# Graph attention, then relational attention: scores of two graphs at a time as four row tiles, and DRAM trips emitted in two steps

## The chip, the cores and the metric

The kernel runs on one core of one Trainium2 chip. The metric is the device time in microseconds of one execution. Before the change it is 2887.8 us, the median of three runs (2886.82, 2887.80 and 2892.35).

## The reference

128 graphs of 128 nodes with 256 features go through two layers. Everything is f32.

- Layer 0: two graph attentions, each a masked softmax of 128x128 additive scores and a product with `h W`; the residual and a layer norm; a feed-forward of 256 to 1024 to 256 with relu; a second norm.
- Layer 1: eight heads of 32 features. The weights of the softmax are masked by relation, and every relation has values of its own:

```
q = src @ Wq + bq; k = src @ Wk + bk           (8 heads of 32)
attn = softmax(q k^T / sqrt(32))
out = sum over r of (attn * (adj == r)) @ (src @ Wv[r] + bv[r])
x = norm(src + out @ Wo + bo)
y = norm(x + gelu(x @ W1 + b1) @ W2 + b2)
```

The adjacency is 0 or 1 in these inputs. The kernel looks for a larger value at its start and has an arm for each case. Here the arm called BINARY runs: the values of relation 0 are applied to all weights, and those of relation 1 less relation 0 to the masked ones, so two products per head remain.

## The kernel before

Graphs are worked on in 32 groups of four (`G`), with the 128 nodes of a graph on the partitions. Every group passes five stages: `load`, `gat` (both graph attentions), `ff0`, `att` (layer 1's attention), `ff1`.

**What sets the order of the work.** Each stage is a Python generator. It emits some instructions and then yields a number of units, which are planned time and not measured time. `layers` (L598) keeps all running stages in a heap by planned time: the stage `k` of group `g` starts at `100 g + begin[k]` (load -87, gat -51, ff0 48, att 132, ff1 300), and each yield puts it back by that many units. So five groups are interleaved, and the pattern repeats every 100 units. The numbers stand in `TIMES` (L30). TensorE (PE) executes in the order of emission from unit 280 on, and SP's queue, which issues every DMA, does so from the start (`kept`, L57). The other engines' order is made by a scheduler at compile time; each of their instructions is placed no earlier than the PE instruction emitted before it. Every engine then takes its own queue in order.

**The trip through DRAM.** To turn 128x128 blocks round, `transposed` (L273) lets VectorE (DVE) transpose 32x32 blocks in place (L288), stores them with four DMAs of 128 KB to a DRAM tile (L291) and loads that tile back with one DMA of 512 KB (L293), in which the blocks stand in their new places. It does the three in one go. In SP's queue the load therefore stands right behind its stores, waits for their landing, and all that is emitted later waits with it. There are seven such trips a group: the features ahead of ff0, att and ff1, and four graphs' weights of attention. `gat_weighting` (L393) has a smaller trip of the same kind (L405, L407). The first and last groups use transposes on PE in some places instead (`direct`, L282).

**PSUM.** Of eight banks, one holds the output `av` of the weighted values, and seven are a pool called `mm` for every other product.

**Attention** (L459). q and k are computed for a group at a time, 512 tokens. ScalarE (ACT) writes k twice for each half of the features into `kbd` (L476), with 32 rows of each 64 set to zero by `own`: a key tile that is block-diagonal over pairs of heads. `weights(b)` (L483) makes the scores of one graph: for each half of the features, two row tiles of 64 rows run side by side, each giving two heads in 256 columns, into two banks. DVE takes the row maxima (L496), ACT the exponentials with their sums (L500), DVE the reciprocals (L501), GpSimd (POOL) the division (L502). `turned` makes the trip. `by_relation` masks (L515), `values` (L525) makes the values and `weighted` (L536) multiplies them with four column tiles of 32 columns; ACT copies the result out (L548), and `wo` (L577) follows. Graph by graph: two graphs' weights are started ahead, and those of graph b+2 are emitted right behind the values of graph b.

**The other stages.** `feed_forward` (L315) computes its first product in eight visits by seven block products in place of eight (L333) and its second product in two halves (L378). A visit of a new unit takes two banks, `chain` and `side`; the second product takes two.

Of the kernel before, what the change touches and what calls it, by code (L numbers as in the profile page):

```python
# [31 lines left out]
    "ff first half": 10, "ff half": 5, "row": 16, "gat": 19, "wh": 5.5,  # L32
    "gat copy": 2, "qk": 4.5, "scores": 5.5, "turn0": 10, "turn1": 5,
    "v0": 5.5, "av": 9, "v": 4, "wo": 4, "turn": 3, "mask": 3,
    "lead ff0": 26, "lead att": 32, "lead ff1": 32, "affine": 7,
# [5 lines left out]
    binary=False, times=TIMES, period=430, bufs=dict(T=3, tok=2, m=4, mm=6, v=1),  # L41
    begin=dict(load=-87, gat=-51, ff0=48, att=132, ff1=300), early={},
# [4 lines left out]
    binary=True, times=TIMES,  # L47
    period=100, bufs=dict(T=5, tok=5, m=1, mm=7, v=2),
# [37 lines left out]
def constants(tc, a, c, cst, tmp, ps):  # L86
# [59 lines left out]
    def others():  # L146
# [16 lines left out]
        c.kbd = [cst.tile([P, G, 2, P], F32, name=f"kbd{n}") for n in range(DC)]  # L163
        c.own = cst.tile([P, 2], F32, name="own")
        nc.vector.memset(c.own, 0.0)
        for q in range(P // Q):
            nc.vector.memset(c.own[ts(q, Q), q % 2:q % 2 + 1], 1.0)
        c.bk_own = [cst.tile([P, DC], F32, name=f"bk{q}") for q in range(2)]
# [52 lines left out]
def stages_of(tc, a, out, c, pools, plan):  # L221
# [51 lines left out]
    def transposed(y, t, direct, z):  # L273
# [4 lines left out]
        if direct:  # L278
# [8 lines left out]
            return  # L287
# [5 lines left out]
        nc.sync.dma_start(t, s.rearrange("k p i t -> p k (i t)"))  # L293
# [4 lines left out]
    def features(y, direct):  # L298

        t = t_tile().rearrange("p (b c n) -> p b c n", b=G, c=DC)  # L300
        blocks = t.rearrange("p b c n -> p (b c) n")
        transposed(y.rearrange("p b (c f) -> p (b c) f", f=P), blocks, direct, blocks)
        return t
# [11 lines left out]
    def feed_forward(y, before, direct, win, bin_, wout, func, by=G):  # L315


        hT = features(y, direct)
# [75 lines left out]
    def gat_weighting(wh, k, cap, direct):  # L394
# [6 lines left out]
        else:  # L401
# [4 lines left out]
            p = e  # L406
            nc.sync.dma_start(p, bass.AP(tensor=s.tensor, offset=s.offset, ap=[[0, P], [1, G * N]]))  # L407
# [51 lines left out]
    def attention(y, g, first, direct):  # L459

        hT = features(y, first or direct)
        at = load_mask(g)
        yield TIMES["lead att"]
        qT = t_tile().rearrange("p (c t) -> p c t", c=DC)
        for i in range(DC):
# [4 lines left out]

        for i in range(DC):
            p = ps.tile([P, G, N], F32, name="mm")
            for f in range(DC):
                nc.tensor.matmul(p, c.wk[:, f, ts(i, P)], hT[:, :, f], start=f == 0, stop=f == DC - 1)  # L474
            for q in range(2):
                nc.scalar.activation(c.kbd[i][:, :, q], p, AF.Identity, scale=c.own[:, q:q + 1],  # L476
                                     bias=c.bk_own[q][:, i:i + 1])
# [5 lines left out]
        def weights(b):  # L483


            scores = [ps.tile([P, DC, 2, N], F32, name="mm") for _ in range(2)]
            for i in range(DC):
                for h in range(2):
                    rows = ts(h, P // 2)
                    nc.tensor.matmul(scores[h][:, i], qT[rows, i, ts(b, N)], c.kbd[i][rows, b],  # L490
                                     start=True, stop=True, tile_position=(h * P // 2, 0))
            e = wk.tile([P, H, N], F32, name="e1")
            for h, p in enumerate(scores):
                p = p.rearrange("p c q n -> p (c q) n")
                nm = sm.tile([P, HC], F32, name="nm1")
                nc.vector.tensor_reduce(nm, p, AX.X, OP.max, negate=True)  # L496
                s = sm.tile([P, HC], F32, name="s1")
                eh = e[:, ts(h, HC)]
                for q in range(HC):
                    nc.scalar.activation(eh[:, q], p[:, q], AF.Exp, bias=nm[:, q:q + 1], accum_out=s[:, q:q + 1])  # L500
                nc.vector.reciprocal(s, s)  # L501
                nc.gpsimd.tensor_mul(eh, eh, per_row(s, N))  # L502
            return e
# [279 lines left out]
```

## Time and profile before

| | |
|---|---|
| median of three runs | 2887.8 us |
| the profiled execution | 2891.83 us, of which span 2890.0 us |
| PE busy | 2787.7 us (96%) |
| ACT, POOL, DVE busy | 1724.3, 1597.4, 1504.7 us |
| share of the DMA engines, main queue | 49.1% |
| granted TensorE clock, mean | 0.982 |

The profile is of one execution. A row of a timeline has the start and the length in us, the engine, the line of the kernel, the operation, what is written from what, the shapes (for PE: rows and columns of the array, then the data) and the number of records; in brackets stands how long the engine was idle before it and what ended that. An f32 matmul is two records. Lengths of matmuls contain their latency, so their pace is read from one start to the next. In the list of waits each line has who waited, for what, the total in us, how often and the longest. SP's rows are DMAs issued, and their length is the time to issue them.

### The profile page before, as it was taken

Reading aid. Unit: us, or ns where it says so; the run is one execution under the profiler, and the core shown is the slowest. Engines: PE = TensorE matmul, PEld = TensorE weight load, DVE = VectorE, ACT = ScalarE, POOL = GpSimd, SP = SyncE. Lnnn points to the kernel's source line nnn. Section 1 sums busy time; section 2 is a strip of 40 time slices with the busy share of each in tenths; the row PEclk is TensorE's granted clock in tenths of the full one; section 3 lists DMA queues with packets and bytes.
Section 4 is the critical chain, followed back from the end, with each engine's and each line's share of the span. In section 5 each row is a group of like instructions: output and inputs, shape, how many; then the busy total and the mean of one; then the engine's idle time right before and its main releaser. Section 6 shows DMA issues by size and latency. Waiting matters only on the chain.

```text
span 2890.0 us, 45554 instructions
## 1 busy us (share of the span) xinstructions
PE 2787.7 (96%) x15554; PEld 2166.1 (75%) x15554; DVE 1504.7 (52%) x3072; ACT 1724.3 (60%) x5191; POOL 1597.4 (55%) x1866
## 2 busy tenths in 40 slices
PE   4996999999999999999999999999999999999988
PEld 3764777777877777777777787777778777777756
DVE  5444545545545555554554555555565545555442
ACT  3445566566666666666656666666666675666543
POOL 1434556556655556665655665565566565556553
PEclk7998999999999999999999999999999999999999
DMA  7145454555554556555445545454654544564310
GB/s 275 45 104 121 104 118 106 110 132 127 119 114 107 113 117 139 114 119 118 106 108 131 129 113 125 104 111 117 137 128 107 123 106 111 122 135 106 77 37 15
DMA packets 1156945, 328.69 MB, mean 114 GB/s; under 512 B 903008, under 2 KB 1126752, under 8 KB 1156064
## 3 DMA queue, kind: packets, MB, share of 16 engines
q1 hardware_dynamic: 1156704, 325.68, 49.1%
q8 instruction: 126, 2.06, 0.3%
q14 instruction: 115, 0.94, 0.1%
HBM read 195.97 MB, written 129.62 MB: 113 GB/s over the span
## 4 chain that ended last, share of the span: by engine, by line
PE 71%; DMA 7%; DVE 6%; POOL 5%; ACT 4%; issue 2%; SPq 2%; DVEq 0%; POOLq 0%; ACTq 0%
PE mm L378 25%; PE mm L333 19%; PE mm L531 5%; PE mm L474 4%; PE mm L468 4%; PE mm L490 4%; PE av L544 3%; PE mm L435 3%; PE mm L577 3%; POOL tok L271 2%; DMA zd<-e 2%; SPq L291 2%; DMA eT<-zd 2%; PE mm L454 1%; DMA zd<-T 1%
## 5 line engine op out<-in xcount | busy, mean ns | idle before, releaser
L271 POOL TENSOR_TENSOR tok<-tok,ln_rows 128x512 f32<-128x512 f32 (+1 forms) x596 | 669.5, 1133 | 34.4 <-PE mm L282 11.1
L500 ACT ACTIVATE e<-mm,nm 128x128 f32<-128x128 f32 x1024 | 362.1, 397 | 239.2 <-DVE nm L496 229.6
L378 PE MATMUL mm<-w,fT 128*128 128x256 f32 x2048 | 460.6, 381 | 0.0
L378 PE MATMUL mm<-wf,fT 128*128 128x256 f32 x2048 | 456.6, 381 | 1.5 <-ACT fT L354 1.5
L378 PEld LDWEIGHTS mm<-w,fT 128*128 128x128 f32 x2048 | 386.6, 190 | 74.2 <-issue 24.2
L502 POOL TENSOR_TENSOR e<-e,s 128x512 f32<-128x512 f32 x256 | 269.4, 1053 | 300.5 <-DVE s L501 299.8
L378 PEld LDWEIGHTS mm<-wf,fT 128*128 128x128 f32 x2048 | 386.5, 190 | 64.3 <-issue 9.2
L515 DVE TENSOR_TENSOR m<-eT,am 128x1024 f32<-128x1024 f32 x128 | 186.2, 1454 | 385.2 <-DMA eT<-zd 374.8
L496 DVE TENSOR_REDUCE nm<-mm 128x4 f32<-128x512 f32 x256 | 162.9, 676 | 254.6 <-PE mm L490 254.6
L265 ACT ACTIVATE tok<-tok,nmr,rstd 128x256 f32<-128x256 f32 x480 | 249.9, 603 | 20.1 <-POOL nmr L263 20.0
L531 PE MATMUL mm<-wv,T 128*128 128x512 f32 x512 | 249.3, 610 | 0.0
L352 POOL TENSOR_TENSOR fT<-fT 128x512 f32<-128x512 f32 x128 | 163.3, 1277 | 153.8 <-ACT fT L351 153.8
L500 ACT ACTIVATION_READ_ACCUMULATOR e<-mm,nm 128x1 f32 x1024 | 242.9, 237 | 0.0
L354 ACT ACTIVATE fT<-fT,col 128x512 f32<-128x512 f32 x256 | 170.4, 715 | 118.8 <-DVE fT L348 117.1
L309 POOL TENSOR_TENSOR t<-T 128x256 f32<-128x256 f32 x64 | 47.6, 744 | 321.3 <-DMA T<-zd 321.0
L333 PE MATMUL mm<-T,w 128*128 128x256 f32 x768 | 202.3, 386 | 4.0 <-DMA T<-zd 2.9
L424 POOL TENSOR_TENSOR e<-e,s 128x512 f32<-128x512 f32 (+1 forms) x68 | 68.1, 1002 | 244.4 <-DVE s L423 230.6
L333 PE MATMUL mm<-T,wf 128*128 128x256 f32 x768 | 193.1, 381 | 0.0
L256 DVE BATCH_NORM_STATS2 st<-tok 128x6 f32<-128x256 f32 x480 | 176.7, 409 | 2.4
L333 PEld LDWEIGHTS mm<-T,w 128*128 128x128 f32 x768 | 144.4, 192 | 30.6 <-issue 6.5
L422 ACT ACTIVATE e<-e,nm 128x128 f32<-128x128 f32 x256 | 101.6, 430 | 105.2 <-DVE nm L419 98.8
L333 PEld LDWEIGHTS mm<-T,wf 128*128 128x128 f32 x768 | 146.1, 191 | 21.7 <-issue 0.8
(144 smaller groups left out, 5147.1 us busy)
## 6 DMA issues: line engine op xcount, KB each, us to landing
zd<-e SPq DMA_DIRECT2D x496, 128.0 KB, 4.6
eT<-zd SPq DMA_DIRECT2D x124, 512.0 KB, 4.4
zd<-T SPq DMA_DIRECT2D x364, 128.0 KB, 3.5
T<-zd SPq DMA_DIRECT2D x91, 512.0 KB, 4.2
xt<-in_xT_dram SPq DMA_DIRECT2D x32, 512.0 KB, 5.0
e<-zsd SPq DMA_DIRECT2D x60, 256.0 KB, 3.3
tok<-in_x_dram SPq DMA_DIRECT2D x30, 512.0 KB
out_dram<-tok SPq DMA_DIRECT2D x29, 512.0 KB, 5.4
```

Source lines behind the costliest of these rows:

```text
L256: nc.vector.bn_stats(st, y[:, b])
L265: nc.scalar.activation(y[:, b], y[:, b], AF.Identity, bias=nmr[:, b:b + 1], scale=rstd[:, b:b + 1])
L271: engine.tensor_tensor(y[:, b:b + n], y[:, b:b + n], v[:, None, :].to_broadcast([P, n, D]), op)
L333: nc.tensor.matmul(p[:, i], win[k][:, ts(f0 + i, P)], hs[k], start=first and i == 0, stop=True, skip_group_check=True)
L352: nc.gpsimd.tensor_add(hi[:, :, 1], hi[:, :, 1], hi[:, :, 0])
L354: nc.scalar.activation(lo[:, i], lo[:, i], func, bias=bin_[:, f0 + i:f0 + i + 1])
L378: nc.tensor.matmul(ys[b // 2][:, b % 2], fT[f][:, ts(b, N)], wout[:, f], start=b % 2 == 0 and n == 0, stop=n == FC - 1, skip_group_check=True)
L496: nc.vector.tensor_reduce(nm, p, AX.X, OP.max, negate=True)
L500: nc.scalar.activation(eh[:, q], p[:, q], AF.Exp, bias=nm[:, q:q + 1], accum_out=s[:, q:q + 1])
L502: nc.gpsimd.tensor_mul(eh, eh, per_row(s, N))
L515: nc.vector.tensor_tensor(m, eT, at[:, b][:, None, :].to_broadcast([P, H, N]), OP.mult)
L531: nc.tensor.matmul(p, hT[:, b, f], wv[:, f, r:r + 2], start=f == 0, stop=f == DC - 1)
```

## The change

Three things change.

1. **Scores.** The key tile is plain: `kT`, one copy per half of the features. `weights(bs)` takes several graphs, two in the BINARY arm (`together=2`). Each matmul has 32 rows and 128 columns, and four row tiles stand side by side, one head each. Head q of a half writes to bank q, which holds two graphs and both halves, so a pair of graphs takes four banks. Four reductions of 128x512 are followed by sixteen exponentials; one reciprocal and one division of 128x1024 follow per graph. The order of the heads in the weights is now the natural one.
2. **Pairs.** The values, masks, output projection and `av` also go by two graphs. The scores of the second pair are emitted right behind the weighted values of the first. The buffers of `m` become two and that of `oT` one, of twice the size.
3. **Two steps.** `transposed` becomes `put` (transpose and stores) and `get` (load). `put` is emitted, 7 units pass, then `get`; for the second graph of a pair 3 more. The gat's small trip is divided by 5 units. The lead times become shorter by as much.

The other arm, GENERAL, which doesn't run here, gets one graph at a time, a longer period and a later ff1.

```diff
-    "ff first half": 10, "ff half": 5, "row": 16, "gat": 19, "wh": 5.5,
-    "gat copy": 2, "qk": 4.5, "scores": 5.5, "turn0": 10, "turn1": 5,
-    "v0": 5.5, "av": 9, "v": 4, "wo": 4, "turn": 3, "mask": 3,
-    "lead ff0": 26, "lead att": 32, "lead ff1": 32, "affine": 7,
+    "ff first half": 10, "ff half": 5, "row": 11, "gat": 19, "wh": 5.5,
+    "gat copy": 2, "qk": 7, "scores": 14, "mask": 4, "av": 8, "wo": 8, "turned": 6,
+    "put": 7, "next put": 3, "row put": 5,
+    "lead ff0": 19, "lead att": 25, "lead ff1": 25, "affine": 7,
...
-    period=100, bufs=dict(T=5, tok=5, m=1, mm=7, v=2),
+    period=100, bufs=dict(T=5, tok=5, m=2, mm=7, v=2),
...
+        return s
+
+    def get(t, s):
+        if s is not None:
+            nc.sync.dma_start(t, s.rearrange("k p i t -> p k (i t)"))
...
-        transposed(y.rearrange("p b (c f) -> p (b c) f", f=P), blocks, direct, blocks)
+        s = put(y.rearrange("p b (c f) -> p (b c) f", f=P), blocks, direct, blocks)
+        yield TIMES["put"]
+        get(blocks, s)
...
+            yield TIMES["row put"]
             nc.sync.dma_start(p, bass.AP(tensor=s.tensor, offset=s.offset, ap=[[0, P], [1, G * N]]))
...
-            for q in range(2):
-                nc.scalar.activation(c.kbd[i][:, :, q], p, AF.Identity, scale=c.own[:, q:q + 1],
-                                     bias=c.bk_own[q][:, i:i + 1])
+            nc.scalar.activation(kT[:, i], p, AF.Identity, bias=c.col["bk"][:, i:i + 1])
...
+        def weights(bs):
+            n = len(bs)
+            scores = [ps.tile([P, n, DC, N], F32, name="mm") for _ in range(HC)]
+            for j, b in enumerate(bs):
+                for i in range(DC):
+                    for q in range(HC):
+                        rows = ts(q, DH)
+                        nc.tensor.matmul(scores[q][:, j, i], qT[rows, i, ts(b, N)], kT[rows, i, ts(b, N)],
+                                         start=True, stop=True, tile_position=(q * DH, 0))
...
+        def turned(es):
+            eT = [wk.tile([P, H, N], F32, name="eT") for _ in es]
+            stored = [put(e, t, direct, e) for e, t in zip(es, eT)]
+            yield TIMES["put"]
+            for n, (t, k) in enumerate(zip(eT, stored)):
+                if n:
+                    yield TIMES["next put"]
+                get(t, k)
             return eT
...
+        STEP = plan["together"]
         yield TIMES["qk"]
+        es = weights(range(STEP))
         yield TIMES["scores"]
+        eT = yield from turned(es)
+        for b in range(0, G, STEP):
+            bs = range(b, b + STEP)
+            vs = [values(k) for k in bs]
+            affine(y, "02", b, STEP)
+            yield TIMES["mask"]
+            parts = [(by_relation(k, e, range(R)), v) for k, e, v in zip(bs, eT, vs)]
             yield TIMES["av"]
+            oT = weighted(parts)
+            if b + STEP < G:
+                es = weights(range(b + STEP, b + 2 * STEP))
             yield TIMES["wo"]
...
+            if b + STEP < G:
+                yield TIMES["turned"]
+                eT = yield from turned(es)
```

## The prediction

> **What bounds the kernel now.** I read the page first: its engine lines, then the 40 slices.
>
> ```profile
> span 2890.0 us, 45554 instructions
> PE 2787.7 (96%) x15554; PEld 2166.1 (75%) x15554; DVE 1504.7 (52%) x3072; ACT 1724.3 (60%) x5191; POOL 1597.4 (55%) x1866
> PE   4996999999999999999999999999999999999988
> ```
>
> TensorE (PE) is full in all slices but the first, the fourth and the last two. A busy share can hide slow matmuls, so I took stretches and then the timeline of PE.
>
> ```profile
> 1000.00:1200.00 200.00, 199.35 (x1118) 156.49 (x1117) 109.35 (x227) 125.74 (x381) 119.72 (x140) 1.00 0.56 124
> 2800.00:2890.00 90.00, 71.17 (x353) 56.43 (x352) 25.88 (x53) 36.00 (x78) 33.94 (x44) 0.89 0.09 24
> ```
>
> (PE, its weight loads, DVE, ACT, POOL, then granted clock, DMA share, GB/s.) In the middle PE idles 0.65 us of 200.
>
> ```profile
> 1063.27 7.07 PE L378 MATMUL mm<-w,fT 128*128 128x256 f32 x32
> 1070.27 1.13 PE L490 MATMUL mm<-kbd,T 64*128 64x256 f32 x8
> 1071.33 0.43 PE L544 MATMUL av<-eT,v 128*32 128x128 f32 x8
> 1071.57 0.40 PE L544 MATMUL av<-m,v 128*32 128x128 f32 x8
> 1072.34 1.13 PE L490 MATMUL mm<-kbd,T 64*128 64x256 f32 x8
> 1073.40 3.72 PE L378 MATMUL mm<-w,fT 128*128 128x256 f32 x16
> 1076.96 1.03 PE L333 MATMUL mm<-T,wf 128*128 128x256 f32 x4
> ```
>
> Starts matter here. Each f32 matmul is two records. A full 256-column record takes 0.2155 us (elsewhere in this answer four of L333 start 0.86 to 0.87 apart). The 32 of L378 take 6.90, and the next start is 7.00 later, so going to a tiled mode costs 0.10. One graph's scores (L490) take 1.06: four pairs of records at 0.216, about 0.10 for the first weights, which nothing hides, and 0.09 of mode change. One graph's values (L544) take 1.01: eight steps of four column tiles at 0.109, 0.03 first weights, 0.09 change. Back in full mode 16 records take 3.56 and not 3.45: 0.11 for exposed weights. PE therefore runs at its own pace, and groups follow each other every 85.1 us (L468 starts at 1056.4 and, a group on, at 1141.4). Last, the waits.
>
> ```profile
> DVE m L515 <- DMA eT<-zd: 374.8, 92, 9.4
> PE av L544 <- DMA eT<-zd: 14.6, 2, 12.0
> SPq L293 <- DMA zd<-e: 327.3, 245, 3.1
> ```
>
> DVE and SP wait long for the trips through DRAM, but PE waited for them only twice, at the ends of the program: the order of emission leaves room.
>
> [...] The trace agrees for two row tiles (two records per 0.216 us); four are not in it. [...] 64-row loads (L490) last 187 ns, 128-row ones (L378) 190, and loads with almost nothing beside them repeat thus:
>
> ```profile
> L192 PEld LDWEIGHTS mm<-col,w 128*128 128x128 f32 x32 | 3.7, 192 | 0.1
> ```
>
> That is 0.112 us each, once the last one's tail is taken off. [...]
>
> **The change part by part, per group of four graphs.**
>
> *Scores.* Before: 4 x 1.06 = 4.24 us. After, a pair is 16 matmuls, 32 records, in 8 steps of four row tiles with 128 columns. A step streams 128 columns (0.109, as in L544) over weights that take 0.112 to load: 0.112. A pair: 8 x 0.112 + 0.10 + 0.09 = 1.09; two, 2.18. Saved 2.06. Bounds: 0.109 a step (saved 2.10), or only two tiles at once, 0.216 (two pairs 3.84, saved 0.40). I take four at once, since row and column tiles already run two and four at once.
>
> *Values and bursts.* Matmuls stay. Before 4 x 1.01 = 4.04; after 2 x (16 x 0.109 + 0.12) = 3.73: saved 0.31. The same timeline, over a whole group, has four tiled bursts (at 1011.7, 1030.4, 1048.2, 1070.3), each costing 0.10 in and 0.11 after; walking the new times gives three: saved 0.2. Output projection and v only change places.
>
> Together **2.57 us a group** of PE.
>
> *Other engines.* Two kbd copies per half (128 of 774 ns) become one kT copy: 49 us less ACT. Reciprocals halve; exponentials, elements of the reductions and POOL's products stay. POOL's affine step goes by two graphs: 1.375 us in place of twice 0.77. None is on the path: PE at 99.7% hides ACT at 60%, POOL and DVE at 55%. Were ACT the bound, the copies would be worth 49/32 = 1.5 us a group.
>
> *Trips.* SP issues the same DMAs. It now runs on past the stores instead of sitting for their landing (327 us for zd<-e alone), so stores of others, xt loads and row trips go earlier; the load stands behind whatever 5 to 7 units emit, the 512 KB output store among it (0.6 us of SP). The lead times keep their sums (7+19=26, 7+25=32, 5+11=16). PE waits for none of these now: nothing gained. Two trips now stand close; the timelines of SP and of DVE give their price:
>
> ```profile
> 1084.28 2.56 SPq L291 DMA_DIRECT2D zd<-e  x4
> 1089.56 0.38 SPq L293 DMA_DIRECT2D eT<-zd  x1
> 1090.04 4.46 SPq L291 DMA_DIRECT2D zd<-e  x4
> 1096.85 0.38 SPq L293 DMA_DIRECT2D eT<-zd  x1
> ```
>
> ```profile
> 1083.02 1.24 DVE L288 STREAM_TRANSPOSE e<-e 128x1024 f32<-128x1024 f32 x1
> ...
> 1093.80 1.85 DVE L515 TENSOR_TENSOR m<-eT,am 128x1024 f32<-128x1024 f32 x1 [2.59 <-DMA eT<-zd]
> ```
>
> Stores take 5.3 us from issue until the load may go (1084.28 to 1089.56), 6.8 when the first load is in their way (1090.04 to 1096.85); a load takes 4.2 (1089.56 to the mask at 1093.80).
>
> *The pair's chain, the new danger.* PE executes in order of emission, so what counts is the PE work between a pair's scores and its values. In units from its group's start, the first pair's scores are emitted at 132+7+25+7 = 171 and its values at 171+14+7+3+4+8 = 207; the second pair's scores follow there, its values at 207+8+6+7+3+4+8 = 243. The other stages repeat every 100 units: the next group's ff0 (from 148) emits the second halves of its second product at 216 and 221, the gat of the group after it (from 149) its last product at 232, the previous group's ff1 (from 200) its first three visits at 237, 239.5 and 242. So between the second pair's scores and values stand: scores with changes 1.2, output projection 8 records 1.72, ff0 32 records 6.90, v of two graphs 8 records of 0.429, 3.43, gat 8 records 1.72, visits of 8, 8 and 12 records 6.03, change 0.09: **21.1 us**. Before it was 35.5 (1012.72 to 1048.20 in the timeline). For the first pair the same walk gives 32. The chain, from the scores' start: scores 1.2; first reduction 0.65; 16 exponentials at 0.35 (eight of L500 go from 1072.15 to 1074.91), 5.6; reciprocal and a product of 1024 elements, twice L502's 1.05 and 0.3, 2.4; transpose 1.2: 11.1 for the second graph. Its stores 5.3 to 6.8, load 4.2, mask 1.2: 21.8 to 23.3. It is needed 0.9 after the first graph's values begin, so the start is allowed at 20.9 to 22.4. PE waits 0 to 1.3 us, and what stands ahead on DVE, ACT or POOL (the gat softmax, a normalisation: up to 2 us, as the mask of 1.85 for 1.22 shows) comes on top: 0 to 3.3. I take 1.0. Behind the waiting matmul PE is in order, so all of it is lost.
>
> *Banks.* Four score banks are held until the sixteen exponentials end. With two of the second product's, six of seven are taken when a feed-forward visit wants two: 0 to 1 us, taken 0.2. The gat rows now queue behind eight stores on SP, with 27 us of PE work to hide them: 0 to 1, taken 0.2. The projection stands 1.2 us behind its values, for ACT's copy of 0.6: 0 to 0.5, taken 0.
>
> *Sum.* 2.57 - 1.4 = 1.17 us a group. From 288 to 2760 us PE is full over 29 periods: 34 us. Start and tail have idle PE and a longer chain by pairs: taken 0, bounds -5 and +8. The profiled execution, 2891.8 (span 2890.0 and 1.8 around it), would be 2858; it stands 4.0 above the median, so **2854**.
>
> **Rivals.** *No stall*: the chain fits; 32 x 2.57 = 82, so 2806 to 2830. For it: the minimum 20.9 is under 21.1, and PE stalls before are 0.2 us a group. Against: any queueing breaks it. *The second pair's values become the bound*, the slower case: eight stores in a row and busy engines bring the operand later than 21.1 + 2.57 = 23.7 us after the scores; from there on the change loses. At 25 it loses 1.3 + 0.4 us a group, 49 us: 2937. For it: the stores of 6.8 us and a DMA share of 0.56; against: the fixed terms end at 22.4. *Row tiles run two at a time*: saved 0.40 + 0.31 + 0.2 = 0.91 less 1.4, 14 us slower: 2902. *Stall eats the gain exactly*: 2888.
>
> **How the numbers follow.** Forecast (2831 to 2880) 0.46; no stall 0.18; gain eaten, within 0.2% (5.8 us, about what a measurement here can tell), 0.07; the chain bound 0.22; two tiles 0.07. Faster 0.64, same 0.07, slower 0.29. The range 2812 to 2905 leaves out about 0.05 below (nothing reaches far under 2806) and 0.14 above. [...]
>
> **What would show it.** Score records of 32 rows, eight per 0.112 us step counting loads, a pair in 1.1; three bursts a group; periods of 83.9. PE idle before the second pair's values, released by the mask or the load eT<-zd, near 1 us; over 2.6 and I am wrong in sign. A step of 0.216 breaks the gain; PE waiting elsewhere, for a bank, means I misplaced the stall. SP's wait for zd<-e should fall well under 327 us without moving PE.

## The result, and the profile after

The changed kernel takes 3101.1 us (median of four runs, 3098.6 to 3105.7) against 2889.2 us (2886.8 to 2892.4): 1.073 times as long, 95% interval 1.0716 to 1.0753. It is 212 us slower, where 2854 us, 34 us faster, was predicted.

The page of the changed kernel begins so (span, engines, PE in 40 slices, then the granted clock in the same slices):

```profile
span 3103.9 us, 46881 instructions
PE 2797.4 (90%) x16578; PEld 2188.5 (71%) x16578; DVE 1505.7 (49%) x2873; ACT 1674.0 (54%) x5063; POOL 1558.1 (50%) x1610
PE   4986999899999999999999999999999899999988
PEclk6997999999999999999999999999999999999999
```

The slices look nearly as full as before: a slice is 78 us, and a few lost microseconds in it don't show. The stretch from 400 to 2600 us shows them. The columns are as in the prediction (PE, its weight loads, DVE, ACT, POOL, granted clock, DMA share, GB/s).

```profile
400.00:2600.00 2200.00, 2030.64 (x12127) 1590.58 (x12126) 1082.83 (x2081) 1230.79 (x3754) 1152.36 (x1176) 0.97 0.49 108
```

The kernel before, in the same stretch:

```profile
400.00:2600.00 2200.00, 2196.31 (x12374) 1714.92 (x12374) 1186.15 (x2430) 1383.42 (x4165) 1292.02 (x1499) 1.00 0.53 119
```

PE idles 169 us here, and 3.7 us before. The groups now follow each other every 92.7 us (median of the starts of the q product), so the stretch holds 23.7 groups, and each has 7.1 us of idle PE. The other engines are less busy in it than before, DVE at 1082.83 us against 1186.15 and ACT at 1230.79 against 1383.42; per group their work is nearly the same or less. No engine became the bound by its sum of work. The page also follows the chain of work that ended last back from the end, and gives each engine's share of the span in it, before and after:

```profile
PE 71%; DMA 7%; DVE 6%; POOL 5%; ACT 4%; issue 2%; SPq 2%; DVEq 0%; POOLq 0%; ACTq 0%
PE 36%; issue 17%; POOL 15%; DMA 13%; ACT 7%; DVE 6%; SPq 5%; POOLq 0%; ACTq 0%; DVEq 0%
```

So the chain leaves PE for long stretches now. The list of PE's waits (who, for what, total us, how often, the longest) tells where the idle time is:

```profile
PE av L557 <- DMA eT<-zd: 96.3, 27, 13.6
PE mm L455 <- POOL e L425: 59.0, 29, 4.5
PE av L557 <- DVE m L526: 34.3, 37, 1.9
PE mm L542 <- ACT wh L445: 23.4, 28, 0.9
PE mm L333 <- ACT fT L339: 21.6, 5, 4.3
```

Four places wait, not one: the weighted values of attention (L557) for their operand, gat's second product (L455) for its softmax, `values` (L542) for a copy on ACT that frees a bank, and the feed-forward visits (L333) for a copy on ACT that takes out a running sum (`chain`) before the next product adds to it. Before, the waits of this list over 7 us lay at the program's ends; between 400 and 2600 us the whole list was one line of 2.8 us.

One group of the changed kernel, PE's timeline around the second pair. Its long wait stands at the feed-forward visits, which is so in five groups; in most it stands right ahead of the values.

```profile
1003.97 1.17 PE L491 MATMUL mm<-kT,T 32*128 32x128 f32 x32
1018.33 1.99 PE L455 MATMUL mm<-wh,e 128*128 128x256 f32 x8 [0.93 <-POOL e L425]
1028.11 2.04 PE L333 MATMUL mm<-t,w1s 128*128 128x256 f32 x4 [4.32 <-ACT fT L339]
1029.94 1.91 PE L333 MATMUL mm<-T,w 128*128 128x256 f32 x4
```

The pair's scores (first row) took 1.10 us to the next start at 1005.07, as predicted. At 1028.11 PE had stood still for 4.32 us. The four records from there took 1.83 us, and the same form takes 0.87 at full clock. The stretches around them, in the form of the stretch from 400 to 2600 us above, show why:

```profile
1023.20:1028.10 4.90, 0.58 (x3) 0.20 (x2) 1.72 (x7) 2.68 (x6) 4.58 (x6) 0.81 0.91 212
1028.10:1033.30 5.20, 5.20 (x14) 3.82 (x14) 2.65 (x5) 1.89 (x4) 0.05 (x1) 0.53 0.58 162
1035.20:1040.00 4.80, 4.80 (x26) 4.24 (x23) 2.34 (x4) 3.81 (x6) 3.34 (x4) 1.00 0.58 91
```

After the wait the granted clock is 0.53 for five microseconds, and then full again. Counted over the trace's clock records between 144 and 2860 us: before, 7 stretches at half clock with 28.8 us of busy PE in them; after, 37 stretches with 160.3 us. The records give a granted clock of 0.5 there; by an estimate from that, half of this busy time is lost, 80 us after and 14 before.

So of the 10.3 us that a group of the changed kernel takes beyond PE's needs at full clock, 7.1 are idle and, by the same estimate, about 2.4 are lost at half clock (from 400 to 2600 us 111.9 us of busy PE lie at a granted 0.5; half of that over 23.7 groups). By place, from start to start of PE's records less their length at full clock (slow matmuls included): values of the second pair 4.9, gat's second product 2.4, feed-forward visits 1.9, `values` 1.1, the rest 0.5, for 0.7 in all before. (The expectations below reckon with 4.6 and 2.0 for the first two.) Of the 4.9, 2.6 lie ahead of the first record; the rest lies within the 64 records, which wait for the second graph's mask and run in part at half clock.

The pair's chain is read from DVE's and SP's timelines. DVE:

```profile
1006.90 0.69 DVE L418 SCALAR_TENSOR_TENSOR e<-e 128x512 f32<-128x512 f32 x1 [8.45 <-ACT e L411]
1007.51 0.68 DVE L495 TENSOR_REDUCE nm<-mm 128x4 f32<-128x512 f32 x1
...
1010.50 0.67 DVE L420 TENSOR_REDUCE nm<-e 128x4 f32<-128x512 f32 x1
...
1015.47 0.18 DVE L424 RECIPROCAL s<-s 128x4 f32<-128x4 f32 x1 [1.32 <-ACT e L423]
...
1030.65 1.23 DVE L526 TENSOR_TENSOR m<-eT,am 128x1024 f32<-128x1024 f32 x1 [5.73 <-DMA eT<-zd]
```

and SP, whose rows are DMAs issued:

```profile
1016.89 6.53 SPq L285 DMA_DIRECT2D zd<-e  x8
1023.52 0.70 SPq L649 DMA_DIRECT2D out_dram<-tok  x1
1024.39 3.23 SPq L291 DMA_DIRECT2D eT<-zd  x2
```

The scores end at 1005.07, but DVE stood in gat's L418, which waited for its row, and came to the first reduction at 1007.51. Three of gat's instructions and the four reductions then alternate. The eight stores start 12.9 us after the scores' start and take 6.5 us to issue; the output's store stands between them and the loads, as predicted. The first load takes 6.3 us to its mask (1024.39 to 1030.65), and 4.2 us was the price from before. The median over all groups, from the scores' start: first reduction 3.65, stores 13.5 to 20.0, load 21.0, values 27.4 us. The first pair of a group (medians over 24 groups from 400 to 2600 us), for which PE doesn't wait, has its first reduction at 1.2, its stores at 11.2 to 17.7, its load at 17.9 and its first mask at 22.9 us, where the second pair's is at 27.3. From the first reduction to the first store both take about 10 us.

What stands behind the pair's softmax is late too. ACT and POOL in the same group (both from their timelines):

```profile
1013.72 0.49 ACT L423 ACTIVATE e<-e,nm 128x128 f32<-128x128 f32 x1
1025.42 2.08 ACT L259 ACTIVATE tok<-tok,nmr,rstd 128x256 f32<-128x256 f32 x4 [9.98 <-POOL nmr L257]
```

```profile
1013.53 3.75 POOL L507 TENSOR_TENSOR e<-e,s 128x1024 f32<-128x1024 f32 x2 [13.42 <-DVE s L506]
1017.24 1.04 POOL L425 TENSOR_TENSOR e<-e,s 128x512 f32<-128x512 f32 x1
```

Gat's exponentials (L423) start at 1013.72, where the sixteen of L504 (1008.23 to 1013.72) end; their operand (DVE's L420) was ready at 1011.17. Gat's division (L425) starts where the two long ones of L507 end, 1.6 us after its operand (L424), and PE's L455 waits for it. On ACT a normalisation (L259) holds the queue for 9.98 us. It waits for POOL's L257, and behind it stand the copies L339 that PE's visit at 1028.11 waits for.

### The profile page after: what moved, and what is told of

The parts are those of the page before. It is cut to its first block, busy times and chain, and to the rows that moved or that the text cites. A ratio compares the mean times of both kernels' runs of the same rounds, so it can differ in the third digit from the quotient of the medians.

```text
span 3103.9 us, 46881 instructions
## 1 busy us (share of the span) xinstructions
PE 2797.4 (90%) x16578; PEld 2188.5 (71%) x16578; DVE 1505.7 (49%) x2873; ACT 1674.0 (54%) x5063; POOL 1558.1 (50%) x1610
## 4 chain that ended last, share of the span: by engine, by line
PE 36%; issue 17%; POOL 15%; DMA 13%; ACT 7%; DVE 6%; SPq 5%; POOLq 0%; ACTq 0%; DVEq 0%
PE mm L333 12%; PE mm L378 10%; DMA eT<-zd 7%; POOL tok L265 6%; SPq L285 4%; ACT e L504 3%; POOL e L507 3%; DMA zd<-e 2%; DVE m L526 2%; PE mm L475 2%; PE mm L470 2%; PE mm L436 2%; PE av L557 2%; DMA e<-zsd 2%; PE mm L584 2%
## 5 line engine op out<-in xcount | busy, mean ns | idle before, releaser
L265 POOL TENSOR_TENSOR tok<-tok,ln_rows 128x512 f32<-128x512 f32 x476 | 628.4, 1334 | 55.2 <-ACT tok L259 33.9
L507 POOL TENSOR_TENSOR e<-e,s 128x1024 f32<-128x1024 f32 x128 | 240.1, 1896 | 826.5 <-DVE s L506 824.1
L504 ACT ACTIVATE e<-mm,nm 128x128 f32<-128x128 f32 x1024 | 358.3, 402 | 219.3 <-DVE nm L495 214.4
L352 POOL TENSOR_TENSOR fT<-fT 128x512 f32<-128x512 f32 x128 | 187.4, 1474 | 355.2 <-ACT fT L351 355.2
L259 ACT ACTIVATE tok<-tok,nmr,rstd 128x256 f32<-128x256 f32 x480 | 249.1, 594 | 154.2 <-POOL nmr L257 143.1
L542 PE MATMUL mm<-wv,T 128*128 128x512 f32 x512 | 238.6, 600 | 23.4 <-ACT wh L445 23.4
L504 ACT ACTIVATION_READ_ACCUMULATOR e<-mm,nm 128x1 f32 x1024 | 248.8, 243 | 0.0
L557 PE MATMUL av<-eT,v 128*32 128x128 f32 x2048 | 122.8, 317 | 96.3 <-DMA eT<-zd 96.3
L333 PE MATMUL mm<-T,w 128*128 128x256 f32 x768 | 209.0, 397 | 0.0
L333 PE MATMUL mm<-T,wf 128*128 128x256 f32 x768 | 192.4, 380 | 0.0
L561 ACT COPY oT<-av 128x512 f32<-128x512 f32 x64 | 37.1, 579 | 284.4 <-PE av L557 284.4
L339 ACT COPY fT<-mm 128x512 f32<-128x512 f32 x128 | 76.8, 600 | 210.5 <-PE mm L333 209.6
L542 PEld LDWEIGHTS mm<-wv,T 128*128 128x128 f32 x512 | 95.5, 191 | 129.0 <-issue 75.4
L418 DVE SCALAR_TENSOR_TENSOR e<-e 128x512 f32<-128x512 f32 (+1 forms) x68 | 44.6, 656 | 276.5 <-ACT e L411 270.9
```

What stands on the lines that cost most here:

```text
L259: nc.scalar.activation(y[:, b], y[:, b], AF.Identity, bias=nmr[:, b:b + 1], scale=rstd[:, b:b + 1])
L265: engine.tensor_tensor(y[:, b:b + n], y[:, b:b + n], v[:, None, :].to_broadcast([P, n, D]), op)
L333: nc.tensor.matmul(p[:, i], win[k][:, ts(f0 + i, P)], hs[k], start=first and i == 0, stop=True, skip_group_check=True)
L352: nc.gpsimd.tensor_add(hi[:, :, 1], hi[:, :, 1], hi[:, :, 0])
L504: nc.scalar.activation(e[:, k], p[:, j, i], AF.Exp, bias=nms[q][:, j, i:i + 1], accum_out=s[:, k:k + 1])
L507: nc.gpsimd.tensor_mul(e, e, per_row(s, N))
```

## The experiments

Two questions are taken in turn: which part of the change costs time, and what the loss by pairs consists of. Ratios are to the kernel before, measured beside each run (2891 to 2895 us). Times of one execution have no interval.

### One part at a time

**Row tiles and the plain key tile alone**, graph by graph, trips in one go:

```diff
-            scores = [ps.tile([P, DC, 2, N], F32, name="mm") for _ in range(2)]
+            scores = [ps.tile([P, DC, N], F32, name="mm") for _ in range(HC)]
...
+                    nc.tensor.matmul(scores[q][:, i], qT[rows, i, ts(b, N)], kT[rows, i, ts(b, N)],
+                                     start=True, stop=True, tile_position=(q * DH, 0))
```

> The kernel before with the plain key tile and four row tiles alone: one graph at a time, trips in one go, all planned times kept. If the row tiles are worth what the profile after shows (a pair of graphs in 1.10 us, so one graph in 0.64 in place of 1.06), 0.42 x 4 x 29 to 32 groups = 49 to 54 us come off: 2835 to 2842. Rival: four score banks of seven a graph, twice as many as before, hold up the other products; then PE waits for banks and the time is 2880 or more.

Measured: 2913.4 us, ratio 1.0076 (1.0046 to 1.0105). The gain of 1.7 us a group isn't there. PE waits at the second graph's scores:

```profile
PE mm L483 <- ACT e L493: 15.7, 60, 2.1
```

From start to start these scores lose 1.6 us a group. The first graph's four banks are held until its exponentials are done, and two graphs want eight of seven banks. So the bank rival's wait is there.

**The same with the second graph's scores 3 units later:**

```diff
-    "qk": 4.5, "scores": 5.5, "turn0": 10,
+    "qk": 4.5, "scores": 8.5, "turn0": 7,
```

> The row tiles of the first experiment (graph by graph, one step), with the second graph's scores 3 units later, behind the first half of the second product's end, so that the first graph's four banks can come free; the trip of the first graph is emitted when it was. If banks ate the row tiles' gain (1.8 us a group of waiting between the first two graphs' scores): 83.6 us a group, 2840 to 2860. If something else did: 2905 to 2920 again.

Measured: 2917.6 us, ratio 1.0087 (1.0058 to 1.0116), not the 2840 to 2860 of the bank theory. The bank wait fell from 15.7 us in 60 places to 3.4 in two, but feed-forward now waits in its place:

```profile
PE mm L327 <- ACT fT L345: 28.8, 29, 1.0
PE mm L372 <- ACT fT L354: 15.3, 28, 0.8
```

A wait was taken away, and larger ones came up at the next stage whose work passes ACT. So the banks alone don't account for the missing gain.

**Row tiles with only graphs 0 and 1 scored together**, in the same four banks, all else graph by graph:

```diff
-        es = [weights(0)]
...
-        es.append(weights(1))
+        es = weights((0, 1))
```

> Row tiles, graph by graph and in one step, but the scores of graphs 0 and 1 made together in the same four banks; graphs 2 and 3 alone. Nothing else goes by pairs. If banks ate the gain: no wait between the first two graphs' scores and one burst less, 2830 to 2850. If any pairing of scores costs what the change cost: above 2930.

Measured: 2960.0 us, ratio 1.0221 (1.0189 to 1.0252), above the 2930 of the second forecast and well slower than the row tiles alone. The wait `PE mm L327 <- ACT fT L345` is now 61.0 us in 29 places. Scoring a pair in one go makes feed-forward's copies late, even with every trip, mask and product of values still by single graphs. L345 copies a running sum out before PE may add to it, so this isn't a wait for a bank. Nor does the copy stand right behind the exponentials. In the 25 waits over 0.5 us between 400 and 2600 us these had ended 16 to 20 us earlier, and in about half of the groups other work, such as gat's L404, runs between the first eight and the second. What held ACT longest ahead of the copy was each time DVE's addition L342, for 2.1 to 4.6 us. In the run with the second graph's scores 3 units later, where eight exponentials run at a time, it was the same addition for 2.25 us. What makes it later with the pair isn't shown.

**Two steps alone**, scores and order as before:

```diff
-            transposed(e, eT, direct, e)
-            return eT
+            return eT, put(e, eT, direct, e)
...
+        yield TIMES["get0"]
+        get(*eT[0])
```

> The kernel before with the trips in two steps alone (load 7 units behind the stores, gat's row load 5 units behind), scores as before, graph by graph, planned times of all PE work kept. Theory 1 (the loss comes from working by pairs): 2880 to 2900, no change. Theory 2 (the loss comes from SP's new order, in which the gat's row load and the loads of the weights stand behind other stores): PE waits 2 us a group or more for the gat's weights and some for eT, 2950 or more.

Measured: 2921.3 us (one execution), 30 us over the kernel before and between the two forecasts. The values wait 40.8 us for the addition to v on DVE (L538), which is later than before. So the two steps weren't free in the old order.

**Pairs with each load right behind its stores:**

```diff
+        get(blocks, s)
         yield TIMES["put"]
-        get(blocks, s)
...
-            stored = [put(e, t, direct, e) for e, t in zip(es, eT)]
+            for e, t in zip(es, eT):
+                get(t, put(e, t, direct, e))
...
```

> The kernel after with every load back behind its own stores, all planned times and with them PE's order kept. Theory 1 (pairs): the second pair's chain is as long as before or longer, since the second graph's stores wait for the first one's load: 3060 to 3130. Theory 2 (SP's order): the 10 us of waiting a group fall to 3 or less, 2900 or less.

Measured: 3160.9 us (one execution), 60 us over the changed kernel and above the 3060 to 3130 of the pairs' theory. The values wait 163.0 us for `eT<-zd`. Within pairs the two steps are worth about 60 us. The rival that SP's new order causes the loss falls.

### What the loss by pairs consists of

**The second pair's values 20 units later**, with their masks and projection:

```diff
+            if b and binary:
+                yield 20
             vs = [values(k) for k in bs]
```

> The kernel after with the second pair's values, masks and products 20 units later (some 17 us more PE work between its scores and its values), nothing else moved. Theory 1 in its form of a chain without cover: the 4.6 us a group that PE waits for eT and m before the second pair's values go, and with them most of the feed-forward's waits: 2930 to 2970. If the waits only move to another place (gat's weights, banks): above 3050.

Measured: 3057.1 us (one execution), so the second forecast came, that the waits move. The wait of the values is nearly gone (11.1 us in all), which took 119 us out of PE's waits, but only 44 us came back. Gat's second product now has the wait:

```profile
PE mm L455 <- POOL e L425: 116.4, 30, 12.4
```

**The same, with the first pair's values (and the second pair's scores behind them) 8 units later**, to let gat's softmax go first:

```diff
-            yield TIMES["av"]
+            yield TIMES["av"] if b or not binary else 16
```

> The kernel after with the second pair's values 20 units later, as before, and now also the first pair's values and with them the second pair's scores 8 units later, so that the gat's second softmax is emitted ahead of the second pair's sixteen exponentials and two long divisions. If it is these that make the gat's weights late (117 us of PE waiting in the run with the later pair): that wait falls under 40 us, 2960 to 2990. If the gat's row trip or DVE's masks make it late: the wait stays near 117 us, 3040 to 3070.

Measured: 3099.6 us (one execution), a miss. Gat's wait went, as expected (9.8 us, for 116.4): in the trace gat's four exponentials now run ahead of the pair's sixteen and its division ahead of the two long ones, in every group from 400 to 2600 us. So it was these that made gat's weights late. But the total rose, and the feed-forward visits have the wait:

```profile
PE mm L333 <- POOL t L309: 118.2, 29, 4.3
```

**The run of exponentials split**: PE's order kept, the second graph's softmax emitted 7 units behind the first's.

```diff
...
-            es = weights(range(STEP))
-            yield TIMES["scores"]
+            es, rest = weights(range(STEP))
+            yield 7
+            for more in rest:
+                more()
+            yield TIMES["scores"] - 7
...
```

> The changed kernel with PE's order kept, where the softmax of each pair's second graph (8 exponentials, reciprocal, product) is emitted 7 units after the first's, so that a run of 16 exponentials on ACT becomes two of 8 with other stages' work let in between. Theory of bunching (the run of 16 exponentials and two long products holds up gat's softmax and feed-forward's copies behind it): gat's second product and feed-forward wait less, by about 2 us a group, while the pair's own chain gets longer by up to 5 us (its banks are held longer too), so the values wait more: 3090 to 3200 in total, the waits of L455 and L333 under half of 59.0 and 21.6 us. Rival, bunching has no part in it: the waits of L455 and L333 stay as they are, and the values' wait grows by the delay alone.

Measured: 3123.0 us (one execution), inside the 3090 to 3200 of the bunching theory. Gat's wait is 31.7 us, for 59.0, just over the half that was asked. Feed-forward's is 5.0 for 21.6. The values wait for `eT<-zd` 158.9 us, for 96.3. The order that was asked for didn't come about, though: the first pair's sixteen exponentials still run in a row, and of the second pair's, fifteen run ahead of gat's four and one behind them. What changed is POOL's order: by the second pair gat's division now stands behind one of the two long divisions and not behind both (all groups from 400 to 2600 us). So gat waits less when less of the pair's softmax stands ahead of it, and the chain of the pair pays for it. What the run of exponentials does to feed-forward isn't tested by this.

**The second pair's scores 8 units earlier**, ahead of the first pair's values:

```diff
+            if b + STEP < G and binary:
+                es = weights(range(b + STEP, b + 2 * STEP))
             yield TIMES["av"]
             oT = weighted(parts)
-            if b + STEP < G:
+            if b + STEP < G and not binary:
```

> The changed kernel with the second pair's scores and softmax emitted 8 units earlier, ahead of the first pair's values instead of behind them; stores, load, masks and values of the second pair stay where they are. Only the distance and the neighbours on DVE and ACT change. Theory of lateness (PE stalls because what stands on the in-order queues of DVE, ACT and POOL comes late): 8 units are some 6.8 us of PE work more between the second pair's scores and its values, and the softmax falls into a stretch where ACT was idle (995.6 to 1004.1 us), so the waits of the values (4.6 us a group) and of gat's second product (2.0) should mostly go, less 0.1 to 0.2 us for a fourth burst: 10.3 - 5 = 5 us of stall a group left, 2940 to 2970 us. Rival, a sum of work that doesn't depend on where the softmax stands (ACT, DVE or the DMA engines too slow for the period): stays within 20 us of 3101. Rival, the wait only moves (as when the values were put later): 3030 to 3090, with gat's or feed-forward's waits taking its place.

Measured: 3029.1 us, ratio 1.0471 (1.0441 to 1.0501). The rival of a sum of work, which had to stay within 20 us of 3101, falls: the same work in another order is 72 us faster. The waits of the values and of gat are small, but two others came:

```profile
PE mm L586 <- ACT oT L561: 69.1, 61, 5.0
PE mm L378 <- DVE v L543: 65.4, 23, 3.8
```

That is the edge of the third forecast, that the wait only moves, with 3030 to 3090.

**Scores ahead of the first pair's masks too**, so that DVE doesn't stand in a mask ahead of the addition to v and of gat's row:

```diff
+            ahead = binary and b + STEP < G
+            if ahead:
+                es = weights(range(b + STEP, b + 2 * STEP))
+                yield 4
             parts = [(by_relation(k, e, range(R)), v) for k, e, v in zip(bs, eT, vs)]
-            yield TIMES["av"]
+            yield TIMES["av"] - 4 * ahead
             oT = weighted(parts)
-            if b + STEP < G:
+            if b + STEP < G and not binary:
```

> As the run with the second pair's scores 8 units earlier, but the first pair's masks are put 4 units later, behind those scores instead of ahead of them (the values stay where they are). In that run DVE stood 2.06 us in the masks waiting for their operand from DRAM, and with it the addition to v (PE waited 65.4 us for it), the store of gat's row and the reductions; gat's late row then held ACT ahead of the copy of the output (PE waited 69.1 us for it). Theory of in-order lateness: with the masks behind, the addition and the row go first, and most of both waits go, 134 us: 2900 to 2940 us, if no new wait takes their place. Rival, the wait only moves again: 2980 to 3030. Rival, the waits have nothing to do with the masks: 3029 as before.

Measured: 2994.9 us, ratio 1.035 (1.032 to 1.038). The wait for the addition to v went, the projection's grew to 91.2 us: the second forecast, that the wait moves (2980 to 3030).

**The same with the second softmax behind the first pair's values:**

```diff
...
             oT = weighted(parts)
...
             if b + STEP < G:
...
+                for more in rest:
+                    more()
...
```

> The same, and the softmax of the second pair's second graph (8 exponentials, reciprocal, product) is emitted behind the first pair's values instead of right behind the first graph's, so ACT's copy of the output stands behind 8 exponentials and not 16. If the run of 16 is what delays the copy and feed-forward's work on ACT: 20 to 50 us under the run without the split. If the copy waits for something else (gat's row): within 10 us of it. If the banks, held longer, now bind: slower than it, with PE waiting in feed-forward's visits or v.

Measured: 2975.2 us, ratio 1.0282 (1.0242 to 1.0323), 20 us less. The gain isn't the one named: the projection still waits 87.6 us, and in the whole trace the sixteen exponentials of a pair still run back to back, so the split wasn't tested here either. What brought the 20 us is open.

**The projection of each pair 5 units later:**

```diff
-            yield TIMES["wo"]
+            yield TIMES["wo"] + 5 * binary
...
-                yield TIMES["turned"]
+                yield TIMES["turned"] - 5 * binary
```

> As the run with scores ahead of the masks and the second softmax split, and the output projection of each pair 5 units later, behind 3.5 us of other PE work (the second pair's stores stay where they are). PE waited 87.6 us there for ACT's copy of the weighted values, which stood behind gat's exponentials and table loads. Theory that pairs lose only by lateness: those 3.5 to 3.8 us a group come back, over 29 groups some 100 us of 2975: 2865 to 2895, at or under the kernel before (2892). Rival, the wait only moves: 2920 to 2975, with feed-forward's visits, v or the values waiting more.

Measured: 2962.9 us, ratio 1.0246 (1.0229 to 1.0263); 2865 to 2895 was hoped for, and the rival's 2920 to 2975 came. The projection's wait fell from 87.6 to 7.7 us, and two others appeared or grew:

```profile
PE mm L333 <- ACT fT L346: 49.5, 27, 2.3
PE av L558 <- DVE m L527: 41.2, 57, 1.8
```

**The second pair's values another 1.5 units later:**

```diff
-            yield TIMES["av"] - 4 * ahead
+            yield TIMES["av"] - 4 * ahead + (1.5 if binary and b else 0)
```

> The same, and the second pair's values (and its projection) another 1.5 units later, 1.3 us more of cover for their masks, which PE waited 1.3 us a group for. Theory of lateness: 20 to 38 us less than the run without it, 2830 to 2870, under the kernel before. Rival, the rest is work or moves: within 10 us of the run without it.

Measured: 2962.4 us, ratio 1.0253 (1.0236 to 1.0270): nothing gained, and the masks are waited for as long as before (40.9 us).

**Filler in the wait.** Four or eight more f32 matmuls of 128x256 stand right ahead of the second pair's values, written to the bank that the values then overwrite:

```diff
+            for _ in range(filler): nc.tensor.matmul(po[:, 0].rearrange("p c n -> p (c n)"), c.wo[:, 0, :P], c.wo[:, 0], start=True, stop=True)
...
```

> The changed kernel with four more f32 matmuls of 128x256 (1.72 us of PE at full clock) right ahead of the second pair's values, on constant operands, into the bank that the values then overwrite: the same waits, part of them filled with work. In the changed kernel the gap there is 3 to 6 us in most groups, and the clock records show half clock for 3.4 or 6.8 us soon after nearly each such gap (160 us of busy PE at half clock in all, 80 us lost). Theory that the fallen clock is a part of the loss: [...] 20 to 60 us less than 3101, with a mean clock over 0.965. Rival, the length of the wait is all: 3095 to 3125, since the filler is hidden in most groups and adds up to 1.7 us in the few where the gap lies elsewhere.

> The same with eight such matmuls, 3.45 us. Theory of the clock: the gaps there are closed nearly whole, so the clock stays, but about half of the groups now wait for the filler: 0 to 60 us less than 3101, mean clock over 0.97. Rival, length is all: 3110 to 3160.

Measured: 3114.1 us with four and 3114.2 us with eight, ratios 1.0763 and 1.0764 (1.0732 to 1.0795), so some 10 us over the changed kernel, with ranges of the ratio that overlap with its own, and with mean clocks of 0.962 and 0.965 for 0.955. Both times lie in the ranges of the rival, that only the length of the wait counts. The clock didn't give the gain that was forecast. The fillers closed the gap ahead of the values (their wait for `eT<-zd` is 40.5 and 23.0 us, for 96.3), but gat's wait rose from 59.0 to 94.4 and 76.1, and the stretches at half clock are still 36 and 30, for 37, with 142.1 and 118.6 us of busy PE in them, for 160.3. So what the fallen clock costs is counted from the records, and not tested by itself. The run shows something else: eight matmuls in each of 30 groups are 30 x 8 x 0.43 = 103 us of PE work, and they cost about 10. (The compile-time order of the other engines shifts a little with them.) PE's own work no longer sets the period. What does isn't one engine's sum of work; in the group from 1000 us the chain that ended last runs through gat's row trip, the exponentials on ACT, the stores, the load `eT<-zd` (6.24 us), the mask and a normalisation, and comes back to PE at the projection at 1041.40.

## Why the prediction was wrong

The saving was forecast rightly, at 2.57 us a group; the loss was put at 1.4 us and is about 10.1. The terms in turn:

*Scores, values and bursts: right.* A pair of scores takes 1.10 us, for 1.09; the four row tiles do run at once, with a step of four starting every 0.112 us (that they would was an estimate, from two row tiles and four column tiles in the trace before); the group has three tiled bursts (at 1002.09, 1033.29 and 1061.44). The work that PE saves is gone, but PE isn't paced by its work any more.

*The pair's chain: the mechanism right, the size wrong.* PE waits at the second pair's values for the load and the mask, as the step said. It was put at 1.0 us with an upper bound of 3.3 and measured 4.9. The fixed terms were summed to an operand at 21.8 to 23.3 us, and the values came at 27.4. Several terms are short. The stores were priced for one graph, but both loads stand behind all eight: already in the first pair, which PE doesn't wait for, the loads go at 17.9 and 20.3 us, where the sum has the second graph's at 16.4 to 17.9. In the second pair the reductions start at 3.65 and not 1.2 us, behind gat's L418; the output's store stands behind the eight, so that the first load goes at 21.0; and it takes 6.3 us to its mask and not 4.2. This mask is 4.4 us later than the first pair's: so much is the "up to 2 us" of others' work ahead.

*Banks: 0.2, measured 1.1, elsewhere and for another reason.* The four score banks, which the term was about, don't hold up the feed-forward visits. The wait stands at `values` (L542), which now makes two graphs' values right behind gat's first product, and it waits for ACT to copy that product out (L445). In the group from 1000 us this is at 1084.40, and the pair's exponentials had freed their banks by 1069. With the row tiles alone the score banks do bind, between the scores of two graphs: 1.6 us.

*Gat's rows: 0.2, measured 2.4.* The place was right and the reason wrong. I put the delay on SP's queue behind eight stores. In the group shown it is on ACT (2.55 us behind the exponentials) and POOL (1.6 us behind two divisions of 1.9 us). With gat's softmax emitted ahead of the pair's, its wait fell from 116.4 to 9.8 us; with one division ahead of it in place of two, from 59.0 to 31.7.

*Other engines: the step that failed.* It said that "None is on the path" because PE at 99.7% hides ACT at 60%, POOL and DVE at 55% (in the window of the 99.7%, 1000 to 1200 us, they are 63, 60 and 55%). In the changed kernel PE's large waits end with ACT, POOL or DVE, or with a load whose stores had to wait for them. A share of busy time says that there is room for the work, and nothing about when it is done. The change left the sums the same or lower and put the work into fewer and longer runs: four reductions, sixteen exponentials, two long divisions, eight stores. In these traces each engine takes its queue in order, as ACT did while its normalisation stood for 9.98 us with the copies behind it, so what stands behind such a run or such a wait is late. Scoring only the first two graphs together, with all else by single graphs, cost 1.45% or 42 us beside the row tiles alone (ratios 1.0221 and 1.0076). Putting the same work of pairs in another order gave back 139 of the 212 us. The feed-forward visits (1.9 us a group) weren't in the sum at all.

*What follows a wait: missing.* "All of it is lost" counts the wait alone. In the trace of the changed kernel the granted clock fell to 0.5 after long gaps on TensorE: within 6 us of the start of each of the 21 gaps over 3 us between 400 and 2600 us a stretch of 3.4 or 6.8 us at half clock begins, and 4 of the ten gaps of 2.0 to 2.7 us have one too. The prediction had no term for it. By the estimate above that is about 2.4 of the 10.3 us a group. It is a share of PE's time and not shown to be a share of the loss, since PE's work no longer sets the period: with eight fillers a group, 103 us more of it, the time rose by about 10 us.

*Trips: "nothing gained".* Wrong on both sides. Alone, the two steps cost 30 us; within pairs they are worth 60 (one execution each). SP's wait for its stores did fall, from 327.3 to 104.4 us.

*Rivals.* "The second pair's values become the bound" was nearest: its rule gives, for values at 27.4 us, 27.4 - 23.7 + 0.4 = 4.1 us a group, 119 us, and 3007. That it comes so near is in part luck: the 27.4 us contain gat's wait and part of the feed-forward's, which stand between the scores and the values, and for which the rule had no term. "No stall", "two at a time" and "gain eaten" fall.

*The sum.* 2.57 - 1.4 became 2.57 less about 10.1 us of new loss; over 29 periods that is 218 us slower, and 212 were measured.

**What stays open.** By moving parts, the loss shrank from 212 to 71 us (3101 to 2962), and every wait that was taken away came back in part somewhere else. Whether some order makes pairs faster than graph by graph isn't settled; no version here beats the kernel before. How the 10 us divide between the long runs and the shorter cover isn't either, since each of these runs changes more than one of them, and no run took the sixteen exponentials apart by themselves.

## What to carry to other kernels

Where one engine is full and all take their queues in order, a busy share of 55% on another engine doesn't say that its work is hidden: ask, for each run of work that a change makes longer, what stands behind it and when the full engine needs that. Read the clock records behind TensorE's waits as well as the waits: in the changed kernel half clock followed all 21 gaps of over 3 us and four of the ten of 2.0 to 2.7 us, with 111.9 us of busy PE in it from 400 to 2600 us. What that costs in time wasn't shown here. And before a saving is put to work by pairs, try the pairing alone on one place, since moving the waits afterwards gave back only part (139 of 212 us).

## What the runs showed of the hardware that was not expected

- Gaps on TensorE (from start to start, beyond the matmul's own length) of 2.1 to 3.5 us were followed by half clock in some cases and not in others. In the changed kernel all 21 of 3.0 us and more were, and four of the ten of 2.0 to 2.7 us. With four fillers 13 of the 17 of 3.0 us and more were, and with the late values two of 3.5 us were not. The stretches of the changed kernel between 400 and 2600 us lasted 3.41 or 6.83 us by the clock records.
- Eight stores of 128 KB in 128-byte pieces took 6.5 us to issue on SP, against 2.5 to 6.1 us for four (median 4.3, before, 400 to 2600 us). The 512 KB load behind eight took 5.5 us to land in the median, and 4.4 us before.
- Four row tiles of 32 rows with 128 f32 columns run side by side: one step of four starts every 0.112 us, which is what one 128-column weight load took alone in the kernel before (L192), and 32 records take 1.10 us, the change of mode and the first weights included.
